# Two graph-attention layers on one core: in layer 0, the edges inside a tile of 128 nodes are summed with a 128x128 block of weights per head

## The chip, the cores and the metric

The kernel is written for one core of a Trainium2 chip. Its time is the device time of one execution in microseconds (us). The engines are named as in the profile: PE (TensorE, with its weight loads on PEld), DVE (VectorE), ACT (ScalarE), POOL (GpSimd) and SP (SyncE, which here only issues transfers). The core has 16 DMA engines.

## The reference

The input is x with 3327 rows of 1024 numbers, and a symmetric 0/1 matrix adj of 3327x3327 with ones on its diagonal; about 0.5% of it is set. Two layers follow, each with a residual and a layer norm. What layer 0 computes, with 8 heads of 128 columns:

```python
h = (x @ W).reshape(C, H, D)
alpha_src = jnp.einsum('hcd,hd->hc', h_heads, a_src)
alpha_dst = jnp.einsum('hcd,hd->hc', h_heads, a_dst)
e = alpha_src[:, :, None] + alpha_dst[:, None, :]
e = jnp.where(e >= 0, e, 0.2 * e)
e = jnp.where(adj[None] == 0, -jnp.inf, e)
attn = jax.nn.softmax(e, axis=-1)
out = jnp.einsum('hij,hjd->hid', attn, h_heads)
x = layernorm(x + out)
```

Layer 1 is the same with one head of 1024 columns, an own W, and a relu on its sum. Output: 3327x1024, float32.

## The kernel before

The nodes are cut into NT = 26 tiles of P = 128 rows (the last one is padded). A node is a *target* where its sum is formed and a *source* where its row of h is used. After the first stage a flag decides between a dense and a sparse program; this input takes the sparse one. All its stages are in an order written out by hand (`manual_schedule`): each engine runs its instructions in the order of the program, and waits only for the data and buffers that it needs.

**Projection and edge lists (L453 to L699).** For each tile, `flip` transposes x (L176), `project` multiplies it with W (L479), and `keep` copies the result out of PSUM on ACT (L491 to L496) and stores a row of HW0 = 1040 numbers per node into `h0_d`: h for 8 heads, and two factors per head (the exponentials of alpha_dst and of 0.2 alpha_dst). Between the matmuls, `pace` advances the generator `listing`, which turns the mask of adj into lists of edges, one tile a round. The steps of a round that matter here:
- `words` (L301): POOL clears the diagonal in the tile's own 128x128 block of the mask (L308), since the edge from a node to itself is handled apart; ACT counts the ones of each row by a copy of the whole mask row with an accumulator (`junk`, L311); DVE packs the mask into words (L318). It runs for the tile four rounds ahead.
- `ends` and `ends2`: PE adds up the counts (L327, L346), ACT copies the sums out (L328, L347), POOL works out the places from them.
- `keys`, `columns` (DVE): the columns of the ones in each row.
- `places`: ACT computes `away` (L384, L385), DVE compares it to form `place` (L391, L392), a matrix of ones which puts each edge into a slot.
- `give` (PE, L401, L411) multiplies with `place`; `take` (ACT, L423 to L428) copies the result out; `sources` (DVE, L436 to L450) makes of it `idx`, the source row of each slot; `tgt` is the target of each slot, `re` a factor of the target per head. A slot with no edge gets an index beyond the table, which the gather drops; for tiles 0 and 1 it gets row 0 instead, so that the buffers hold finite numbers.

**Layer 0 (class `Layer0`, pipelined by `pipeline`).** Each tile has NB = 17 gathers of 128 rows (L803, POOL, indirect DMA): EB = 4 batches of NG = 4, each of the four for 32 of the tile's targets, and one for what is left (`end`). Five `src` buffers hold the batches in turn. For a batch, `weights` computes on DVE and ACT the weight of each slot and head (L865 to L868) and multiplies it with the one-hot rows `oh` of its targets into `e` (L870; three buffers); `sums` multiplies `e` with the gathered rows on PE (L898, for the last batch L882), and the one-hot rows with the weights for the denominators (L907, L886). While the sums of batch b run, `weights` of the next is issued ahead of them, and the same batch of the next tile is fetched behind them. The edge of a node to itself is added by `own`: its weight `es` is computed on DVE (L845 to L847), ACT scales the tile's own rows with it (L850), and PE adds the scaled rows through an identity matrix (L890). `finish` divides (L918 to L924), applies the layer norm, computes the scores of layer 1 (L931), and stores the row into `y_d`.

**Layer 1 (class `Target`)** gathers from `y_d` with the same `idx`, sums with L993, and multiplies with W afterwards (L1025).

Of the kernel before, what the change touches and what calls it, by code (L numbers as in the profile page):

```python
# [9 lines left out]
F32 = mybir.dt.float32  # L10
BF16 = mybir.dt.bfloat16
U8 = mybir.dt.uint8
# [7 lines left out]
P = 128  # L20
# [6 lines left out]
def kernel(  # L27
# [84 lines left out]

    cnt = const.tile([P, NT, 3], F32, name="cnt")
    loop = const.tile([P, NT], F32, name="loop")


    idx = const.tile([P, NT, NB], I32, name="idx")
# [162 lines left out]
    class Edges:  # L280
# [20 lines left out]
        def words(self, ad, junk):  # L301

            sbuf, ph, t = self.ph.sbuf, self.ph, self.t
            own = ad[:, t * P : (t + 1) * P].bitcast(mybir.dt.int8)
            nc.gpsimd.affine_select(  # L308
                out=own, in_=own, pattern=[[1, P]], compare_op=OP.not_equal, fill=0.0, base=0, channel_multiplier=-1
            )  # L310
            nc.scalar.activation(junk, ad, AF.Copy, accum_out=self.deg)  # L311
            self.deg_b = sbuf("deg_b", [P, 1], 4, dt=BF16)
            nc.scalar.activation(self.deg_b, self.deg, AF.Copy)
            w = ad.bitcast(I32)
            for n in range(3):
                m = WD >> n
                half = sbuf(f"wd{n}", [P, m], 4 if n == 2 else 1, dt=I32)
                nc.vector.scalar_tensor_tensor(  # L318
                    half, w[:, m:], 1 << n, w[:, :m], op0=OP.logical_shift_left, op1=OP.bitwise_or
                )  # L320
# [132 lines left out]
    with ExitStack() as own, tc.manual_schedule():  # L453
# [112 lines left out]
        nc.vector.memset(masks[4], 0.0)  # L566
        nc.vector.memset(masks[4][:, :1], 1.0)
        junk = pool.tile([P, NP], U8, bufs=1, name="junk")
        junk_h = pool.tile([P, DH], BF16, bufs=1, name="junk_h")
        def score_column(k):  # L570

# [171 lines left out]
    def sparse(own):  # L743
# [12 lines left out]
        way = bank("E", [P, HALF], "way")  # L756
        ident_b = pool.tile([P, P], BF16, name="ident_b")
        nc.vector.tensor_copy(ident_b, ident)
        none_b = pool.tile([P, 1], BF16, name="none_b")
        nc.vector.memset(none_b, 0.0)  # L760
        io_t = ph.iota([P, P], [[1, P]], "io_t", base=1)
# [35 lines left out]
        listed = {}  # L797
        last = nc.gpsimd.to_reg(NP - 1)

        def gather(table, w, t, b):  # L800
            s = srcs[(t * EB + b) % NS] if b < EB else ends[t % 2]
            for g in range(NG if b < EB else 1):
                nc.gpsimd.indirect_dma_start(  # L803
                    out=s[:, g, :w], out_offset=None, in_=table[:, :],
                    in_offset=bass.IndirectOffsetOnAxis(ap=idx[:, t, b * NG + g : b * NG + g + 1], axis=0),
                    bounds_check=last, oob_is_err=False,
                )
# [6 lines left out]
        def marks(t):  # L814
# [4 lines left out]
            nc.vector.tensor_tensor(  # L819
                parts[0], io_t[:, :GT].unsqueeze(1).to_broadcast([P, m, GT]),  # L820
                tgt[:, t, :m].unsqueeze(2).to_broadcast([P, m, GT]), OP.is_equal,
            )
            nc.vector.tensor_scalar(parts[1], io_t, tgt[:, t, m:], None, op0=OP.is_equal)
            return parts

        class Layer0:
# [4 lines left out]

            def prepare(self):
                self.re = listed.pop(self.t)
                self.oh, self.oh2 = marks(self.t)
# [17 lines left out]
            def begin(self):  # L852
                self.acc = [bank("A", [P, 4, DH], "acc") for _ in range(2)]

            def fetch(self, b):
                self.src[b] = gather(h0_d, HW0, self.t, b)

            def weights(self, b):

# [16 lines left out]
            def sums(self, b):  # L876
# [9 lines left out]
                    nc.tensor.matmul(self.den, self.oh2, w[:, 0, :], start=False, stop=True)  # L886
                    return

                if b in (1, 2):
                    nc.tensor.matmul(  # L890
                        self.acc[b - 1].rearrange("p h d -> p (h d)"), ident, self.h[:, (b - 1) * HALF : b * HALF],
                        start=False, stop=False,
                    )
                elif b == 3:
                    nc.tensor.matmul(self.acc[0][:, 0, :1], ident_b, none_b, start=False, stop=False)
                for h in range(H):
                    for g in range(NG):
                        nc.tensor.matmul(  # L898
                            self.acc[h // 4][g * GT : (g + 1) * GT, h % 4, :], e[:, g, h, :], rowsof[:, g, h, :],
                            start=first and h % 4 == 0, stop=False,  # L900
                        )
# [38 lines left out]
        class Target:  # L940
# [5 lines left out]
            def prepare(self):  # L946
# [7 lines left out]
                self.oh, self.oh2 = marks(t)  # L954
                self.res = ys[t % 3]
                nc.sync.dma_start(self.res, y_d[t * P : (t + 1) * P, :])

# [8 lines left out]
                nc.vector.tensor_tensor(es[:, :1], es[:, 1:], loop[:, t : t + 1], OP.mult)  # L966

            def fetch(self, b):
                self.src[b] = gather(y_d, HW, self.t, b)

            def begin(self):
                self.acc = [bank("A", [P, CUTS[1]], "acc1") for _ in range(3)]
# [259 lines left out]
```

## Time and profile before

| | us |
|---|---|
| Time, median of 3 runs | 1955.56 (1948.99 to 1957.19) |
| The profiled execution, its own time | 1903.19 |
| Span of the profile | 1901.5 |
| Busy: PE / PEld / DVE / ACT / POOL | 1518.5 / 902.4 / 1146.6 / 546.6 / 1030.2 |
| Gathers of layer 0 on POOL (L803, 416 of them) | 441.1 |
| Sums of layer 0 on PE (L898) | 278.5 |
| Projection on PE (L479) | 402.3 |
| First gather of layer 0, first gather of layer 1 | at 482.3, at 1198.6 |

The times of all rows come from one profiled execution, which was 52 us shorter than the median of the runs. A group of instructions is shown as: line, engine, operation, written tile, read tiles, partitions x elements, count; then busy time in us and mean duration in ns; then the engine's idle time just before them and what ended most of it. A wait is shown as: who waited, for whom, us in total, how often, the longest.

### The profile page before, as it was taken

What the parts mean: (1) busy time and instruction counts of PE and PEld (TensorE: products, weight loads), DVE (VectorE), ACT (ScalarE), POOL (GpSimd) and SP (SyncE); (2) the same over time, 40 slices, a digit from 0 to 9 for tenths busy, and PEclk for the clock granted to TensorE, in tenths of its full rate; (3) what the DMA queues carried; (4) which work ended last, traced back from release to release, by engine and by line L of the source; (5) the groups of instructions that cost most, each with busy time, mean ns of one, the idle gap of its engine ahead of it and who ended that gap; (6) DMA issues with size and microseconds to landing.
All of it is one profiled execution on the core that took longest, in us unless ns stands there. A gap on an engine that the chain in (4) does not pass through costs nothing.

```text
span 1901.5 us, 38079 instructions
## 1 busy us (share of the span) xinstructions
PE 1518.5 (80%) x14663; PEld 902.4 (47%) x14663; DVE 1146.6 (60%) x3058; ACT 546.6 (29%) x1422; POOL 1030.2 (54%) x1391
## 2 busy tenths in 40 slices
PE   8799999999266555656556565399999999999997
PEld 5465556666255554545545454144444444444443
DVE  6699999986386665666666666244444444444442
ACT  5544455542022222222222222012222212222220
POOL 4322222220576666676676764677766667666650
PEclk9899999999678777787788877699999999999999
DMA  7656455411899999999999997899999999999980
GB/s 184 101 133 131 100 99 99 88 62 39 325 373 404 396 392 394 366 405 392 386 392 389 394 376 273 332 398 410 400 372 382 380 378 369 359 371 373 366 326 33
DMA packets 171068, 567.76 MB, mean 299 GB/s; under 512 B 27690, under 2 KB 34346, under 8 KB 170878
## 3 DMA queue, kind: packets, MB, share of 16 engines
q0 software_dynamic: 131056, 455.68, 67.6%
q1 hardware_dynamic: 39822, 109.56, 15.4%
q8 instruction: 118, 1.93, 0.4%
q14 instruction: 72, 0.59, 0.1%
HBM read 578.85 MB, written 42.97 MB: 327 GB/s over the span
## 4 chain that ended last, share of the span: by engine, by line
PE 52%; DMA 24%; DVE 12%; ACT 6%; issue 4%; POOL 2%; SPq 0%; DVEq 0%; ACTq 0%; POOLq 0%
DMA src<-h_d,idx 20%; PE mm L1025 20%; PE acc L993 12%; PE mm L479 12%; DVE e L870 3%; PE acc L898 3%; ACT junk L311 3%; PE tr L176 2%; POOL src L803 2%; DMA src<-y_d,idx 2%; DVE pr L931 1%; PE acc L882 1%; DMA wt<-in_L_gnn_W_dram 1%; ACT xT L179 1%; PE xp L411 1%
## 5 line engine op out<-in xcount | busy, mean ns | idle before, releaser
L803 POOL DMA_INDIRECT src<-h_d,idx x416 | 441.1, 1060 | 209.1 <-PE acc L898 58.0
L803 POOL DMA_INDIRECT src<-y_d,idx x416 | 415.7, 999 | 221.6 <-PE acc L993 96.3
L898 PE MATMUL acc<-src,e 128*32 128x128 f32 x6656 | 278.5, 337 | 253.6 <-DVE e L870 253.5
L479 PE MATMUL mm<-wt,xT 128*128 128x347 f32 (+1 forms) x1248 | 402.3, 469 | 3.3 <-DMA wt<-in_L_gnn_W_dram 2.9
L1025 PE MATMUL mm<-wt,xT 128*128 128x512 f32 x832 | 383.3, 604 | 0.8 <-DVE o L1028 0.8
L898 PEld LDWEIGHTS acc<-src,e 128*32 128x32 f32 x6656 | 234.8, 137 | 311.3 <-DVE e L870 284.3
L479 PEld LDWEIGHTS mm<-wt,xT 128*128 128x128 f32 x1248 | 228.3, 192 | 106.0 <-issue 4.2
L1025 PEld LDWEIGHTS mm<-wt,xT 128*128 128x128 f32 x832 | 152.2, 190 | 199.5 <-issue 179.1
L993 PE MATMUL acc<-src,es 128*32 128x342 f32 (+1 forms) x2496 | 206.2, 464 | 33.8 <-DVE es L984 31.0
L870 DVE TENSOR_TENSOR e<-oh,way 128x1024 f32<-128x1024 f32 x130 | 158.7, 1221 | 63.2 <-ACT w L868 62.8
L993 PEld LDWEIGHTS acc<-src,es 128*32 128x32 f32 x2496 | 71.6, 111 | 158.6 <-issue 112.9
L868 ACT ACTIVATE w<-way 128x32 f32<-128x32 f32 (+1 forms) x130 | 24.6, 189 | 407.7 <-DVE way L866 395.6
L1028 DVE SCALAR_TENSOR_TENSOR o<-mm,y 128x512 f32<-128x512 f32 x52 | 35.9, 691 | 166.2 <-PE mm L1025 166.2
L1007 ACT ACTIVATE z<-y,ri 128x342 f32<-128x342 f32 (+1 forms) x78 | 39.5, 570 | 313.9 <-DVE ri L1003 313.9
L865 DVE TENSOR_TENSOR way<-src,re 128x32 f32<-128x32 f32 x104 | 20.8, 200 | 175.1 <-DMA src<-h_d,idx 157.6
L179 ACT ACTIVATE xT<-tr 128x512 f32<-128x512 f32 x104 | 59.4, 596 | 151.0 <-PE tr L176 150.9
L981 DVE TENSOR_TENSOR way<-way,src 128x128 f32<-128x128 f32 x104 | 31.1, 299 | 90.0 <-ACT way L951 44.2
L850 ACT ACTIVATE own<-own,es 128x128 f32<-128x128 f32 x208 | 63.6, 388 | 57.4 <-DVE es L847 57.4
L311 ACT ACTIVATE junk<-ad 128x3328 uint8<-128x3328 uint8 x26 | 78.4, 3014 | 2.5 <-POOL ad L308 2.5
L882 PE MATMUL acc<-end,e 128*128 128x128 f32 x416 | 67.7, 328 | 13.3 <-DVE e L870 13.3
L296 POOL CAST mvs<-r 128x8 bf16<-128x8 f32 x26 | 6.0, 232 | 122.8 <-ACT r L295 122.8
L335 POOL TENSOR_TENSOR place_of<-cnt 128x1 f32<-128x1 f32 x26 | 4.9, 190 | 121.0 <-ACT cnt L328 101.5
(188 smaller groups left out, 1959.7 us busy)
## 6 DMA issues: line engine op xcount, KB each, us to landing
h_d<-ht SPq DMA_DIRECT2D x26, 520.0 KB
own<-h_d SPq DMA_DIRECT2D x26, 520.0 KB
y_d<-y SPq DMA_DIRECT2D x26, 514.0 KB
y<-y_d SPq DMA_DIRECT2D x26, 514.0 KB
x<-in_x_dram SPq DMA_DIRECT2D x25, 512.0 KB
y<-in_x_dram SPq DMA_DIRECT2D x25, 512.0 KB
out_dram<-o SPq DMA_DIRECT2D x25, 512.0 KB
ad<-in_adj_dram POOLq DMA_DIRECT2D x25, 415.9 KB
```

Of the source, the lines that this page charges most:

```text
L176: nc.tensor.transpose(tr[:, k, :], src[:, (4 * g + k) * P : (4 * g + k + 1) * P], ident)
L179: nc.scalar.activation(part, tr, AF.Copy)
L311: nc.scalar.activation(junk, ad, AF.Copy, accum_out=self.deg)
L479: nc.tensor.matmul(acc, xT[t][:, k, :], wt[:, k, CUTS0[c] : CUTS0[c + 1]], start=k == 0, stop=k == KT - 1)
L803: nc.gpsimd.indirect_dma_start(out=s[:, g, :w], out_offset=None, in_=table[:, :], in_offset=bass.IndirectOffsetOnAxis(ap=idx[:, t, b * NG ...
L850: nc.scalar.activation(hn, hn, AF.Copy, scale=es[:, n : n + 1])
L870: nc.vector.tensor_tensor(e, oh.unsqueeze(2).to_broadcast([P, ng, H, wide]), wp.unsqueeze(3).to_broadcast([P, ng, H, wide]), OP.mult,)
L882: nc.tensor.matmul(self.acc[h // 4][:, h % 4, :], e[:, 0, h, :], rowsof[:, 0, h, :], start=False, stop=h % 4 == 3,)
L898: nc.tensor.matmul(self.acc[h // 4][g * GT : (g + 1) * GT, h % 4, :], e[:, g, h, :], rowsof[:, g, h, :], start=first and h % 4 == 0, stop= ...
L993: nc.tensor.matmul(self.acc[c][to, :m], es[:, g, :], s[:, g, CUTS[c] : CUTS[c + 1]], start=b == 0, stop=b == EB,)
L1007: nc.scalar.activation(z[:, cut], self.res[:, cut], AF.Copy, scale=ri[:, 1:2])
L1025: nc.tensor.matmul(acc, xT[:, k, :], wt1[:, k, half], start=k == 0, stop=k == KT - 1)
```

## The change

The edges inside a tile, the one from each node to itself among them, leave the gathers of layer 0 and are summed from the tile's own rows of h, which are loaded in any case. For this:
- in `words`, ACT copies the tile's 128x128 block of the mask into `block` (bf16) before POOL clears the diagonal;
- in `ends`, PE transposes `block`, and ACT stores it as `near` (sources by targets, one byte each), which stays in SBUF;
- `outside` finds the slots whose source lies in the tile (DVE, four small operations), sets their target to 0, so that no one-hot row matches them, and for tiles from 2 on moves their index beyond the table;
- `own` and `own_half` make per head a block `el` of weights: PE transposes the broadcast factor of the targets, four heads at a time, ACT forms Relu(r a - b), DVE adds b and multiplies with `near`; `el` takes one of the three `e` buffers;
- `sums` of batch 1 has 8 matmuls with `el` over the own rows for the sums and 8 with a column of ones for the denominators, instead of L890 on batches 1 and 2; `finish` no longer adds `es`.

Layer 1 keeps its lists. The core of the diff:

```diff
@@ words
-            own = ad[:, t * P : (t + 1) * P].bitcast(mybir.dt.int8)
+            own = ad[:, t * P : (t + 1) * P]
+            self.block = sbuf("block", [P, P], 4, dt=BF16)
+            nc.scalar.activation(self.block, own, AF.Copy)
+            own = own.bitcast(mybir.dt.int8)
             nc.gpsimd.affine_select(
...
@@ ends
+            tb = self.ph.bank("T", [P, P], "tb", BF16)
+            nc.tensor.transpose(tb, self.block, self.ph.same)
+            nc.scalar.activation(near[:, self.t, :], tb, AF.Copy)
             op = self.ph.bank("T", [P, 1], "op")
...
+        def outside(t):
+
+            inside = sbuf("inside", [P, NB], 2)
+            nc.vector.tensor_scalar(inside, idx[:, t, :], float(t * P), None, op0=OP.is_ge)
+            nc.vector.scalar_tensor_tensor(
+                inside, idx[:, t, :], float((t + 1) * P), inside, op0=OP.is_lt, op1=OP.mult
+            )
+            to = sbuf("far_t", [P, NB], 3)
+            nc.vector.scalar_tensor_tensor(to, inside, 0.0, tgt[:, t, :], op0=OP.is_equal, op1=OP.mult)
+            rows_of = idx[:, t, :]
+            if t > 1:
+                rows_of = sbuf("far_i", [P, NB], 3, dt=I32)
+                nc.vector.scalar_tensor_tensor(
+                    rows_of, inside, float(NONE), idx[:, t, :], op0=OP.mult, op1=OP.add
+                )
+            far[t] = rows_of, to
...
         def get_edges(t):
+            for n in (0, 1) if t == 0 else (t + 1,):
+                if n < NT:
+                    outside(n)
...
@@ Layer0.own
-                es = self.es = sbuf("es0", [P, H], 2)
-                nc.scalar.activation(es, sd0[:, t, 0, :], AF.Exp, scale=1 - SLOPE)
-                nc.vector.tensor_tensor(es, es, h[:, D : D + H], OP.mult)
-                nc.vector.tensor_tensor(es, es, h[:, D + H :], OP.max)
-                nc.vector.tensor_scalar(es, es, loop[:, t : t + 1], None, op0=OP.mult)
-                for n in range(H):
-                    hn = h[:, n * DH : (n + 1) * DH]
-                    nc.scalar.activation(hn, hn, AF.Copy, scale=es[:, n : n + 1])
+                r, nb = sbuf("es0", [P, H], 2), sbuf("nb0", [P, H], 2)
+                nc.scalar.activation(r, sd0[:, t, 0, :], AF.Exp, scale=1 - SLOPE)
+                nc.vector.tensor_scalar(nb, h[:, D + H :], -1.0, None, op0=OP.mult)
+                self.el = sbuf("e", [P, H * P], 3, "el").rearrange("p (h t) -> p h t", h=H)
+                self.rn = r, nb
+                self.own_half(0)
+
+            def own_half(self, g):
+                t, h, e = self.t, self.h, self.el
+                r, nb = self.rn
+                tr = bank("T", [P, 4, P], "tr")
+                for n in range(4):
+                    nc.tensor.transpose(
+                        tr[:, n, :], r[:, 4 * g + n : 4 * g + n + 1].to_broadcast([P, P]), ident
+                    )
+                for n in range(4 * g, 4 * g + 4):
+                    nc.scalar.activation(
+                        e[:, n, :], tr[:, n % 4, :], AF.Relu, bias=nb[:, n : n + 1], scale=h[:, D + n : D + n + 1]
+                    )
+                    nc.vector.scalar_tensor_tensor(
+                        e[:, n, :], e[:, n, :], h[:, D + H + n : D + H + n + 1], near[:, t, :],
+                        op0=OP.add, op1=OP.mult,
+                    )
...
@@ Layer0.sums
-                if b in (1, 2):
-                    nc.tensor.matmul(
-                        self.acc[b - 1].rearrange("p h d -> p (h d)"), ident, self.h[:, (b - 1) * HALF : b * HALF],
-                        start=False, stop=False,
-                    )
-                elif b == 3:
+                if b == 1:
+                    for h in range(H):
+                        nc.tensor.matmul(
+                            self.acc[h // 4][:, h % 4, :], self.el[:, h, :], self.h[:, h * DH : (h + 1) * DH],
+                            start=False, stop=False,
+                        )
+                elif b > 1:
                     nc.tensor.matmul(self.acc[0][:, 0, :1], ident_b, none_b, start=False, stop=False)
...
+                if b == 0:
+                    self.own_half(1)
...
+                if b == 1:
+                    for h in range(H):
+                        nc.tensor.matmul(
+                            self.den[:, h : h + 1], self.el[:, h, :], one, start=False, stop=False
+                        )
...
@@ Layer0.finish
-                nc.vector.tensor_tensor(ri, self.den, self.es, OP.add)
-                nc.vector.reciprocal(ri, ri)
+                nc.vector.reciprocal(ri, self.den)
```

The gathers of layer 0 take their indices from `far[t][0]`, its one-hot rows their targets from `far[t][1]`; those of layer 1 stay with `idx` and `tgt`.

More of the change, by code (lines that the diff above doesn't have):

```diff
@@ L114 @@
     loop = const.tile([P, NT], F32, name="loop")
+    near = const.tile([P, NT, P], U8, name="near")
     idx = const.tile([P, NT, NB], I32, name="idx")
@@ L568 @@
         junk = pool.tile([P, NP], U8, bufs=1, name="junk")
+        ph.same = pool.tile([P, P], BF16, bufs=1, name="same")
+        nc.vector.tensor_copy(ph.same, ident)
         junk_h = pool.tile([P, DH], BF16, bufs=1, name="junk_h")
@@ L758, in sparse @@
         nc.vector.tensor_copy(ident_b, ident)
+        one = pool.tile([P, 1], F32, name="one")
+        nc.vector.memset(one, 1.0)
         none_b = pool.tile([P, 1], BF16, name="none_b")
@@ L798, in sparse, with gather @@
         last = nc.gpsimd.to_reg(NP - 1)
-        def gather(table, w, t, b):
+        far = {}
+        def outside(t):
[13 more added lines that the diff above has]
+            far[t] = rows_of, to
+        def gather(table, w, t, b, rows_of):
             s = srcs[(t * EB + b) % NS] if b < EB else ends[t % 2]
@@ L804, in gather @@
                     out=s[:, g, :w], out_offset=None, in_=table[:, :],
-                    in_offset=bass.IndirectOffsetOnAxis(ap=idx[:, t, b * NG + g : b * NG + g + 1], axis=0),
+                    in_offset=bass.IndirectOffsetOnAxis(ap=rows_of[:, b * NG + g : b * NG + g + 1], axis=0),
                     bounds_check=last, oob_is_err=False,
@@ L810, in get_edges, with marks @@
         def get_edges(t):
+            for n in (0, 1) if t == 0 else (t + 1,):
+                if n < NT:
+                    outside(n)
             listed[t] = sbuf("re", [P, NB, H], 3)
             nc.sync.dma_start(listed[t], re_d[t])
-        def marks(t):
+        def marks(to):
             m = NB - 1
@@ L820, in marks @@
                 parts[0], io_t[:, :GT].unsqueeze(1).to_broadcast([P, m, GT]),
-                tgt[:, t, :m].unsqueeze(2).to_broadcast([P, m, GT]), OP.is_equal,
+                to[:, :m].unsqueeze(2).to_broadcast([P, m, GT]), OP.is_equal,
             )
-            nc.vector.tensor_scalar(parts[1], io_t, tgt[:, t, m:], None, op0=OP.is_equal)
+            nc.vector.tensor_scalar(parts[1], io_t, to[:, m:], None, op0=OP.is_equal)
             return parts
@@ L833, in prepare @@
                 self.re = listed.pop(self.t)
-                self.oh, self.oh2 = marks(self.t)
+                self.oh, self.oh2 = marks(far[self.t][1])
                 self.y = ys[self.t % 3]
@@ L855, in fetch @@
             def fetch(self, b):
-                self.src[b] = gather(h0_d, HW0, self.t, b)
+                self.src[b] = gather(h0_d, HW0, self.t, b, far[self.t][0])
             def weights(self, b):
@@ L953, in prepare @@
                 )
-                self.oh, self.oh2 = marks(t)
+                self.oh, self.oh2 = marks(tgt[:, t, :])
                 self.res = ys[t % 3]
@@ L968, in fetch @@
             def fetch(self, b):
-                self.src[b] = gather(y_d, HW, self.t, b)
+                self.src[b] = gather(y_d, HW, self.t, b, idx[:, self.t, :])
             def begin(self):
```

## The prediction

> **What bounds the kernel now.** I read the slices of the page first (part 2; 40 slices of 47.5 us).
>
> ```profile
> PE   8799999999266555656556565399999999999997
> DVE  6699999986386665666666666244444444444442
> PEclk9899999999678777787788877699999999999999
> DMA  7656455411899999999999997899999999999980
> ...
> L898 PE MATMUL acc<-src,e 128*32 128x128 f32 x6656 | 278.5, 337 | 253.6 <-DVE e L870 253.5
> L870 DVE TENSOR_TENSOR e<-oh,way 128x1024 f32<-128x1024 f32 x130 | 158.7, 1221 | 63.2 <-ACT w L868 62.8
> ```
>
> Three stages show: up to about 480 us PE and DVE are full (projection and edge lists); from 482 to 1198 us the DMA row is full (layer 0); after that PE and DMA both are (layer 1). The change touches the first two. The busy-time windows give their sizes (columns: busy us of PE, PEld, DVE, ACT, POOL with counts, clock, DMA share, GB/s).
>
> ```profile
> 100.00:460.00 360.00, 350.21 (x2387) 215.61 (x2385) 326.13 (x917) 172.71 (x477) 81.23 (x377) 1.00 0.46 97
> 500.00:1150.00 650.00, 392.20 (x7637) 327.16 (x7635) 414.67 (x996) 157.25 (x463) 441.75 (x419) 0.79 1.01 390
> ```
>
> In layer 0 the DMA share is 1.01 at 390 GB/s while PE has 40% and DVE 36% free: bytes bound it. In projection PE is 97% busy and DVE 91%. The waits from 60 to 460 us tell what PE's last 3% wait for, and the timeline of one round of the edge lists why.
>
> ```profile
> PEld L411 <- DVE place L391: 29.6, 21, 7.9
> ...
> PE xp L411 <- DVE place L391: 18.0, 14, 7.3
> ...
> DVE place L391 <- ACT away L384: 16.1, 19, 4.2
> ```
> ```profile
> 209.04 0.29 POOL L308 TENSOR_SCALAR_AFFINE_SELECT ad<-ad 128x128 int8<-128x128 int8 x1
> ...
> 209.66 0.57 DVE L318 SCALAR_TENSOR_TENSOR wd<-ad 128x416 int32<-128x416 int32 x1
> ...
> 209.95 0.22 ACT L428 ACTIVATE tgt<-xp 128x1 f32<-128x1 f32 x1
> 210.00 3.02 ACT L311 ACTIVATE junk<-ad 128x3328 uint8<-128x3328 uint8 x1
> ...
> 213.14 0.20 ACT L313 ACTIVATE deg_b<-cnt 128x1 bf16<-128x1 f32 x1
> ...
> 214.00 0.73 ACT L384 ACTIVATE away<-io_q,place_of 128x512 f32<-128x512 f32 x1
> ...
> 214.76 0.49 DVE L391 TENSOR_SCALAR place<-away,cnt 128x512 bf16<-128x512 f32 x1 [0.64 <-ACT away L384]
> ```
>
> One round is a closed loop: PE's placing matmuls (L411, L401), ACT's copies (to L428), ACT's row count over the mask (`junk`, 3.02), ACT's `away`, DVE's `place`, PE's next L411. POOL's clearing of the diagonal (L308) is off it: it ended 0.67 us before ACT and 0.33 before DVE (L318) needed the mask. PE waits for `place` in 14 of 25 rounds and is just in time in most others, so what lengthens this loop lengthens the stage.
>
> [...] granted clock 0.79 in layer 0, and 64 matmuls of L898 took 3.64 us after a gap of 4.04 us, 1.95 us without one. More PE work in layer 0 should therefore partly pay for itself.
>
> **Layer 0: bytes removed.** The reference's mask has 53,496 edges off the diagonal; 2,120 of them (4.0%) lie within a tile. Tiles 0 and 1 keep theirs as gathers (rows_of is changed for t > 1 only), so 1,960 rows of 4,160 bytes go: 8.15 MB, at 390 GB/s **20.9 us**. That an index past the end moves nothing shows in the page: software_dynamic moved 455.68 MB, while 56,576 slots a layer at 4,160 and 4,112 bytes would be 468 MB without the mask loads. The number of gathers on POOL stays 17 a tile; each takes 0.99 and 0.30 to the next, 21.9 us a tile.
>
> A tile now takes 26.3 us (mean step of L918) and would take 25.5. Work per tile on the others:
> - PE: now 392.2/650 x 26.3 = 15.9. Added: eight f32 transposes (L176: eight in 1.03 warm, 1.97 cold), 1.5; eight block matmuls (L882, same shape, 67.7/26) 2.6; eight sums of one column with full weights (L886, 0.29 each) 2.3. Removed: L890 twice, 1.1. Sum 21.2, 83% of 25.5.
> - DVE: now 16.8. Added: eight masked multiplies (L924, eight in 2.16) 2.2, four small operations in `outside` (L447, 0.17) 0.7, one for nb 0.2; removed four of some 0.2. Sum 19.1.
> - ACT: eight Relu instead of eight scaled copies (L850, 2.44), even.
>
> All stay under 25.5, so the DMA hides them, but the coupling is tighter. DVE's half 0 waits for transposes queued behind the last tile's sums, half 1 for those behind sums(0); `el` takes one of three `e` buffers, so the `e` of batch 3 waits for sums(1). Sums(1) ends some 5 us later (4 matmuls of half 1, den, and DVE's 1.2), and with it the refill of its src buffer. The chain shows gathers of 9 to 14 us from issue to landing against some 6.3 us for a batch, so one to two batches are queued: 5 us fit once a tile, if recovered. Uncovered are the start (from 520 to 545 us the chain runs through DVE pr L773 and e L870) and the last tile (own lands at 1166 and everything follows it): 2 us each. Layer 0: -20.9 + 4 = **-17**; bounds -21 and, with half the gain lost to drained queues, -6.
>
> **Projection: a wait added.** ACT copies the block before POOL clears the diagonal, and ACT's `junk` and DVE's L318 still wait for POOL. Now L308 starts only after ACT's tgt copies. Price: block copy 0.29 (L425, same tile, 0.285), hand-over 0.08 (L328 ends at 250.28, POOL's L335 starts at 250.36), L308 0.29, hand-over 0.08: 0.74 us in which ACT has nothing else. Queued behind on ACT: junk, deg_b, `away`, and often the copies of project (L496). On DVE, L318 moves to 210.74, by 1.08; `sources` and `places` are behind it; on POOL, the next mask load and factors, both early. In the shown round `away` moves by 0.74, DVE is ready at 215.20, earlier than `away` at 215.47, and place comes 0.74 later. So I read 22 rounds from 85 to 413 us: +0.7 in most, +0.3 in three where DVE was the later, 0.85 to 1.3 in four where L318 stood first. Sum 17. Start-up has two words in a row on ACT (65.8, 69.0): +0.7. The bf16 transpose in `ends` is on PE inside the loop: L346's row beside it costs under 0.1, L176's transpose 0.13; 26 x 0.1 = 2.6. The `near` copy (0.29) falls where ACT waits 2 to 4 us for L327; cnt goes 0.3 later, and POOL has 2.4 to spare before L346. Projection: **+20**; from below 8 (if the last rounds, where PE is 100% busy, and the rounds just in time absorb it), from above 28 (if DVE's later start adds to ACT's). Layer 1 and the tables of ACT are unchanged: 0.
>
> **Sum.** 1903.19 (the profiled execution, span 1901.5) - 17 + 20 = 1906. The runs shown have a median of 1955.56, 2.7% above it; I carry the difference over: 1958.6, said as 1958. Where those runs lose 52 us no view shows; if to slower transfers, the saving is a little larger.
>
> **Rivals.**
> 1. The added wait is hidden (*faster*). For it: several rounds have PE just in time, and PE is 100% busy from 400 to 460. Against it: 18.0 us of waits for `place`. With +5 in projection: -17 + 5 = -12, some 1943. Chance 0.22.
> 2. The gain of layer 0 is half lost (*slower*): later refills of src drain the DMA queue at each tile's start. Decides if sums(1) runs over by more than the queue's 1 to 2 batches (6 to 12 us). For it: own work crosses PE, ACT, DVE and PE twice, and POOL needs 5.2 us to issue a batch. Against it: DVE waits 156.9 us for src in this stage, 6.3 a tile. -6 + 20 = +14, 1970. Chance 0.22.
> 3. PE bounds layer 0 (*slower*): at a clock as low as in the cold bursts (3.64 for 1.95) 21.2 becomes over 25.5 from a factor of 1.2 on. At 27.5 a tile: 24 x 1.2 = +29, with +20: 2005. Against it: the clock should rise. Chance 0.11.
> 4. That indices are not dropped: unlikely, as existing empty slots are marked in the same way; +24, in rival 2's chance.
>
> **Numbers.** The likeliest case, 0.45, is no change: 1958, its own range 1947 to 1968. A measurement of this kernel tells from no change about 0.5%, 10 us. Faster by more 0.22, within 0.43, slower by more 0.35. The range 1938 to 1986 takes in rivals 1 and 2 and the bounds (-21 + 8 = -13 and -6 + 28 = +22) with some width for the runs, and leaves out rival 3.
>
> **What would show it.** Right: projection ends near 500 us instead of 480; ACT idle before `junk` of 0.4 to 0.5 by POOL in each round, and L411's wait for `place` up by some 15 us; layer 0 from first gather to the first of layer 1 some 699 us instead of 716, DMA share still 1.0, clock above 0.79. Wrong: a DMA share below 0.97 in layer 0 (rivals 2, 3), PE over 95% there (3), or projection longer by under 8 us (1).

## The result and the profile after

The changed kernel takes 2035.87 us (median; 2030.36 to 2038.57), the kernel before beside it 1956.38 (1948.99 to 1958.43): a ratio of 1.0392, 95% interval 1.0365 to 1.0419. It is slower by 79.5 us, outside the predicted range (1938 to 1986).

The slices and the sums of layer 0 on the page after, as shown of before (40 slices, now of 50.8 us):

```profile
PE   8799999998478878888878878369999999999997
...
DVE  6688888886576766675576666424444444444342
...
PEclk9899999999678788787787887769999999999999
DMA  7555445410989999999999999499999999999980
...
L948 PE MATMUL acc<-src,e 128*32 128x128 f32 x6656 | 375.9, 325 | 126.9 <-issue 114.4
```

The group L948 is L898 of before: the same 6,656 matmuls. Before, PE stood idle ahead of them for 253.6 us and waited for DVE's `e`, which waited for rows. Now 114.4 of its 126.9 us of idle time end on "issue": on nothing that the profile shows. The busy time rose from 278.5 to 375.9 us while the mean of one went from 337 to 325 ns: the matmuls did not become longer, they overlap less. The DMA row still shows nines in layer 0; the windows below tell more.

The windows of the kernel after (columns as before):

```profile
100.00:460.00 360.00, 336.12 (x2256) 206.57 (x2254) 309.52 (x865) 178.30 (x503) 84.92 (x380) 0.99 0.45 96
500.00:1150.00 650.00, 502.83 (x7276) 403.53 (x7278) 417.76 (x1074) 149.86 (x404) 379.67 (x372) 0.79 0.93 336
```

In layer 0 the transfers went from 390 to 336 GB/s, and the share from 1.01 to 0.93. Bytes are no longer the bound. The gathers by `src` give the stages (first and last start in us):

```profile
L834 POOL DMA_INDIRECT src<-y_d,idx x416: 984/991/1487, 1307.8 to 1973.0; - x139
...
L834 POOL DMA_INDIRECT src<-h_d,idx x32: 986/990/2012, 507.1 to 558.6; - x32
```

Layer 0 ran from 507.1 to 1307.8, 801 us, against 716 before; the projection ended 25 us later. The waits of layer 0 in the kernel after (507 to 1308 us) put the largest one on PE's weight loads:

```profile
PEld acc L948 <- issue: 210.9, 337, 2.0
...
PE acc L948 <- issue: 114.4, 233, 1.8
DVE el L896 <- issue: 110.2, 18, 9.1
```

PE's timeline shows what such a wait looks like. These are the weight loads inside one batch's sums; from 858 to 861 us the granted clock is 1.00:

```profile
857.30 0.18 PEld L948 LDWEIGHTS acc<-src,e 128*32 128x32 f32 x3 [0.52 <-issue]
858.03 0.19 PEld L948 LDWEIGHTS acc<-src,e 128*32 128x32 f32 x5 [0.54 <-issue]
858.75 0.14 PEld L948 LDWEIGHTS acc<-src,e 128*32 128x32 f32 x2 [0.54 <-issue]
859.49 0.11 PEld L948 LDWEIGHTS acc<-src,e 128*32 128x32 f32 x1 [0.60 <-issue]
860.20 0.19 PEld L948 LDWEIGHTS acc<-src,e 128*32 128x32 f32 x5 [0.60 <-issue]
860.92 0.11 PEld L948 LDWEIGHTS acc<-src,e 128*32 128x32 f32 x1 [0.54 <-issue]
```

PE does a handful of weight loads with their matmuls in 0.2 us, stands for 0.55, and goes on, each 0.73 us after the last. Over the stage, some 160 such steps are 0.7 to 0.8 us apart and some 50 twice that (how many depends on where a pause is taken to begin); three to four weight loads of each are recorded, and some records are missing. The data of all 32 matmuls were there, since one `e` and one `src` serve them all. DVE's "issue" ahead of `el` is of another kind: in the timeline ACT's `el` begins 0.49 us earlier (at 629.78, DVE's at 630.27) after a wait of its own for PE, and DVE follows it. Only PE's waits have no visible cause.

Of the 79.5 us, 25 are thus the projection's. The other 55 lie in layer 0 and behind it. How they divide can't be read: the kernel before has no trace at its 1956 us, and its profile of 1903 us has next to none of these waits. Set 2 below has both kernels with the waits.

### The profile page after: what moved, and what is told of

It reads as the page before. It is cut to its first block, busy times and chain, and to the rows that moved or that the text cites. A ratio compares the mean times of both kernels' runs of the same rounds, so it can differ in the third digit from the quotient of the medians.

```text
span 2033.2 us, 40346 instructions
## 1 busy us (share of the span) xinstructions
PE 1737.7 (85%) x15651; PEld 1060.5 (52%) x15651; DVE 1214.8 (60%) x3292; ACT 575.7 (28%) x1474; POOL 1020.8 (50%) x1391
## 3 DMA queue, kind: packets, MB, share of 16 engines
q0 software_dynamic: 131056, 447.53, 64.7%
q8 instruction: 125, 2.05, 0.4%
## 4 chain that ended last, share of the span: by engine, by line
PE 72%; issue 9%; ACT 7%; DVE 6%; DMA 3%; POOL 2%; another core or an unknown queue 2%; SPq 0%; POOLq 0%; DVEq 0%; ACTq 0%
PE mm L1081 17%; PE acc L948 17%; PE mm L487 12%; PE acc L1049 11%; PE acc L931 4%; PE acc L940 3%; ACT junk L316 3%; PE tr L178 2%; PE den L965 2%; PE tr L889 1%; POOL src L834 1%; DMA wt<-in_L_gnn_W_dram 1%; DMA src<-h_d,idx 1%; PE den L959 1%
## 5 line engine op out<-in xcount | busy, mean ns | idle before, releaser
L834 POOL DMA_INDIRECT src<-h_d,far_i x384 | 391.7, 1020 | 287.9 <-PE acc L948 117.8
L948 PE MATMUL acc<-src,e 128*32 128x128 f32 x6656 | 375.9, 325 | 126.9 <-issue 114.4
L487 PE MATMUL mm<-wt,xT 128*128 128x347 f32 (+1 forms) x1248 | 409.7, 475 | 3.4 <-DMA wt<-in_L_gnn_W_dram 2.3
L948 PEld LDWEIGHTS acc<-src,e 128*32 128x32 f32 x6656 | 250.2, 129 | 227.7 <-issue 210.9
L1049 PE MATMUL acc<-src,es 128*32 128x342 f32 (+1 forms) x2496 | 212.3, 466 | 39.4 <-DVE es L1040 26.9
L896 DVE SCALAR_TENSOR_TENSOR el<-el,own,near 128x128 f32<-128x128 f32 x208 | 70.6, 351 | 205.3 <-issue 110.2
L893 ACT ACTIVATE el<-tr,nb,own 128x128 f32<-128x128 f32 x208 | 78.3, 457 | 263.3 <-PE tr L889 156.4
L931 PE MATMUL acc<-end,e 128*128 128x128 f32 x416 | 81.8, 375 | 2.4 <-DVE e L919 2.0
L1057 DVE TENSOR_TENSOR ri<-acc,es 128x1 f32<-128x1 f32 x26 | 4.1, 158 | 125.6 <-PE acc L1049 112.8
L931 PEld LDWEIGHTS acc<-end,e 128*128 128x128 f32 x416 | 74.9, 278 | 4.8 <-DVE e L919 2.1
```

What stands on the lines that cost most here:

```text
L487: nc.tensor.matmul(acc, xT[t][:, k, :], wt[:, k, CUTS0[c] : CUTS0[c + 1]], start=k == 0, stop=k == KT - 1)
L834: nc.gpsimd.indirect_dma_start(out=s[:, g, :w], out_offset=None, in_=table[:, :], in_offset=bass.IndirectOffsetOnAxis(ap=rows_of[:, b * NG ...
L893: nc.scalar.activation(e[:, n, :], tr[:, n % 4, :], AF.Relu, bias=nb[:, n : n + 1], scale=h[:, D + n : D + n + 1])
L896: nc.vector.scalar_tensor_tensor(e[:, n, :], e[:, n, :], h[:, D + H + n : D + H + n + 1], near[:, t, :], op0=OP.add, op1=OP.mult,)
L931: nc.tensor.matmul(self.acc[h // 4][:, h % 4, :], e[:, 0, h, :], rowsof[:, 0, h, :], start=False, stop=h % 4 == 3,)
L948: nc.tensor.matmul(self.acc[h // 4][g * GT : (g + 1) * GT, h % 4, :], e[:, g, h, :], rowsof[:, g, h, :], start=first and h % 4 == 0, stop= ...
```

## The experiments

They ran in five sets. Each set has its own runs of the kernel before, and kernels are compared within a set, because the kernel before took 1898.52, 1987.57, 1901.48, 1902.76 and 1899.60 us in them; sets 2 and 3 were on the same chip, a quarter of an hour apart. Stages in us, from the profiles by first gathers:

| Run | Set | Ratio (95%) | Projection to | Layer 0 | Rest |
|---|---|---|---|---|---|
| e1, before | 1 | 1 | 479.3 | 710.7 | 704.7 |
| e3, `el` in a buffer of its own | 1 | 1.0054 (1.0037 to 1.0071) | 504.1 | 696.8 | 702.8 |
| e4, block copied by POOL | 1 | 0.9951 (0.9935 to 0.9968) | 488.1 | 699.2 | 700.6 |
| e6, before | 2 | 1 | 482.3 | 779.5 | 735.4 |
| e5, after | 2 | 1.0370 (1.0348 to 1.0391) | 505.6 | 813.0 | 739.6 |
| e7, lists only | 2 | 0.9999 (0.9982 to 1.0016) | 482.7 | 769.4 | 732.8 |
| e8, block, all gathered | 2 | 1.0352 (1.0317 to 1.0387) | 501.1 | 815.5 | 740.5 |

Only set 2 shows PE's waits; the profile of the recorded result shows them too. In the texts below, theory C is that PE's instructions come late while transfers fill the DMA engines, and that the change gives PE more of them; the other theories are named in each text.

### Set 1: the parts that the prediction had priced

**e1: the kernel before.** 

> The kernel before, unchanged, with a profile on the chip of the other runs of this set. The first profile of it was 52 us shorter than its timed runs. Theory A (layer 0 of the changed kernel is bound by PE, whose work grew and whose instruction supply stalls): here a step of layer 0 stays 26 to 27 us and PE's sums wait for DVE's e, not for nothing (issue). Rival (stalls of PE with no waited-for engine are there before the change as well, and the first profile was a lucky one): the profile shows 100 us and more of L898 waiting on issue and a step near 28 us.

Measured: 1896.42 us. Its window 560 to 1140 us in layer 0:

```profile
560.00:1140.00 580.00, 350.48 (x7042) 293.54 (x7046) 370.01 (x906) 147.14 (x430) 399.90 (x381) 0.82 1.01 394
```

That is the picture of the first profile: the transfers bound it. None of PE's matmuls waits on "issue" in it.

**e2: more PE instructions.** The kernel before with

```diff
+                if b:
+                    for _ in range(13 if b < 3 else 12):
+                        nc.tensor.matmul(self.acc[0][:, 0, :1], ident_b, none_b, start=False, stop=False)
```

> The kernel before, with 37 more matmuls of one bf16 column per tile in layer 0 (the L895 kind, adding zeros), so that PE issues about as many instructions per tile as in the changed kernel (348 matmuls for 311) with little added busy time (under 0.1 us each, some 3 us a tile, where PE waits 9.5 us a tile for e). Theory A1 (PE is held by the supply of its instructions): a step of layer 0 goes from 26.3 towards 29 us, the time up by 50 us or more. Theory A2 (PE is held by its busy time alone): up by less than 10 us, since the wait for e takes the 3 us in.

The loops add 38 matmuls in a tile (988 in the trace, for 26 tiles), so 76 instructions with their weight loads, and all of them in layer 0. The texts here and below that say 37 and 74, or "each layer", are off by that.

Measured: ratio 0.9997 (0.9988 to 1.0007). In the window from 560 to 1140 us 861 of the added matmuls take 32.59 us of PE's busy time, 0.04 us each. With the transfers as the bound, 76 more instructions of PE in a tile are free.

**e3: `el` not in `e`'s buffers.** The kernel after with

```diff
-                self.el = sbuf("e", [P, H * P], 3, "el").rearrange("p (h t) -> p h t", h=H)
+                self.el = sbuf("z", [P, D], 3, "el").rearrange("p (h t) -> p h t", h=H)
```

> The changed kernel with el in buffers of its own (those that layer 1 uses for z), so that it no longer takes one of the three e buffers. Theory A (PE-bound): the step of layer 0 stays at 29.4 us, the time within 10 us of the changed kernel (2035). Rival B (the coupling through the e buffers holds DVE and so PE): the step falls by 2 us or more, the time by 50 us or more.

Measured: 1.0054; layer 0 696.8 us, 14 less than e1 and only 2 less than e4, where `el` shares `e`'s buffers. The sharing costs next to nothing.

**e4: POOL copies the block.** The kernel after with

```diff
-            nc.scalar.activation(self.block, own, AF.Copy)
+            nc.gpsimd.tensor_copy(self.block, own)
```

> The changed kernel with the copy of the 128x128 block made on POOL, in front of its clearing of the diagonal, instead of on ACT. By the prediction's step for projection ACT no longer waits for POOL between tgt and junk: the stage gives back 14 to 17 of the 20 us, the time falls to some 2018 to 2021. Rival (the added length of projection is PE's transposes and the T buffers): less than 5 us come back. Layer 0 is not touched and should stay at 29.4 us a step.

Measured: 0.9951, faster than the kernel before. The projection ends at 488.1 and not at 504.1 as in e3, whose projection is that of the changed kernel: ACT's place in the order was worth 16 us. Layer 0's gain of 11.5 us stays.

### Set 2: the changed kernel where PE waits

**e5 and e6: both kernels again.** 

> The changed kernel, unchanged. In the set before, the kernel before took 1898.5 and the changed kernel with the block copied on POOL 1889.3, so Theory C (the large loss of the recorded result, 2035.87 against 1956.38, needs a chip or a condition in which PE lacks instructions in layer 0; without it the prediction's sum holds) expects 1905 beside a before of 1898, ratio 1.000 to 1.008, and L948 waiting on issue for under 10 us; in the other condition 1.035 to 1.043, with 200 us of that wait, and a before of some 1956. Theory A (PE-bound by its own work on every chip): ratio near 1.04 beside any before.

> The kernel before, with a profile on the same chip as the run above. If that run shows the stalls of PE, this one tells what they cost the kernel before: Theory C expects its L898 to wait on issue too, for less (50 us or more), and a step of layer 0 of 27.5 to 28.5 us; if the run above shows none, 26.2 us a step and under 20 us on issue.

Measured: 1.0370. The same window of the kernel before (e6) and of the changed one (e5), and the waits of e6 in it:

```profile
560.00:1140.00 580.00, 430.99 (x6346) 294.66 (x6347) 342.30 (x837) 135.74 (x398) 357.69 (x346) 0.84 0.97 359
```
```profile
560.00:1140.00 580.00, 467.41 (x6667) 370.86 (x6668) 369.41 (x954) 138.32 (x367) 336.05 (x327) 0.80 0.94 330
```
```profile
PEld acc L898 <- issue: 237.8, 356, 1.5
...
PE acc L898 <- issue: 132.0, 302, 1.7
```

The kernel before has the waits as well: layer 0 takes 779.5 us, 69 more than in e1, with the same matmuls. The change did not make them; it meets them. (Of the 102 us between the profiles of e1 and e6, 31 lie behind layer 0; no run shows their cause.)

What bounds layer 0 is another engine here. In e6 PE is busy for 430.99 of the 580 us and idle on "issue" for 138.2; everything else that it waits for comes to 8.3. In e5 the three are 467.41, 100.9 and 6.9. And the wait for rows, which bounds e1, is nearly gone in e6. Over the whole run, first e1, then e6:

```profile
DVE way L865 <- DMA src<-h_d,idx: 162.8, 66, 7.8
```
```profile
DVE way L865 <- DMA src<-h_d,idx: 21.1, 4, 8.7
```

Of the 61 us between the profiles of e6 and e5, 23 lie in the projection, 33 in layer 0 and 4 behind. (e6's profiled execution was 11 us above its median, so by the medians layer 0 lost up to 44.)

**e7: lists without the edges inside a tile.** The kernel before with `outside` and its lists, and its old `own`. 

> The kernel before, with only the lists of layer 0 shortened as in the change: the slots inside a tile get no target and, from tile 2 on, no index. It leaves out the edges inside a tile other than the own one. The prediction's first step (8.15 MB at 390 GB/s): 20.9 us less than before, 1878 beside 1898, a step of 25.5 us. If PE's instruction supply binds, 0 to 5 us less.

Measured: 0.9999. So 8.15 MB fewer bytes and `outside` on DVE give nothing here, and cost nothing. The row packets do take longer in e6 than in e1 (an estimate from their share of the 16 engines in the window, 81.5% for 49,520 packets and 84.4% for 54,516: 153 and 144 ns each), but slower transfers that bound layer 0 would make fewer bytes worth more, not nothing.

**e8: the block, and all rows gathered.** The kernel after with

```diff
-            if t > 1:
+            if t > NT:
```

> The changed kernel with every index left in its gathers, so that the block does the in-tile sums while their rows still arrive (without a target). Where the bytes bind layer 0: 20.9 us more than the changed kernel. Where PE binds it (theory A, or C in its second condition): within 4 us of the changed kernel.

Measured: 1.0352 (1.0317 to 1.0387), the interval of e5. Its window has 341 GB/s, e5's 330: the bytes are moved again and the time is the same. The cost is that of the block and of ACT's wait; the saved bytes are worth nothing in this set.

### Sets 3 to 5: what are PE's waits?

These were to tell three causes apart beside a kernel before that waits. In all three sets it did not, so they tell what the change is worth without the waits, and leave the cause open.

**e9, e14, e18: the edit of e2 three times more.** 

> The kernel before with 37 one-column matmuls more in each tile of each layer (zeros added: the values are unchanged), 74 instructions of TensorE more a tile and about 1.5 us more of its busy time. The same edit as in the run e2, where TensorE hardly waited for its own instructions. The question is what the waits are that TensorE shows in layer 0 as waiting for nothing. Theory C (its instructions come late while the rows' transfers fill the DMA engines): on a chip where the kernel before shows 200 us or more of such waits in layer 0, the added instructions cost by their number, 74 of some 700 a tile, so 1.5 to 3 us a tile and the ratio 1.02 to 1.045. Rival (what counts is TensorE's busy time alone): 1.5 us a tile at the most where it is the bound and its waits unchanged, ratio 1.00 to 1.02, and the same as the kernel with wide matmuls. Where the kernel before has few such waits: ratio 1.00 again.

> The kernel before with 37 one-column matmuls more in each tile of each layer, 74 instructions of TensorE and about 1.5 us of its busy time more a tile (values unchanged). Without TensorE's waits: ratio 1.000, as twice before. With them: theory C (late instructions) 1.5 to 3 us a tile in layer 0, where the waits are, 40 to 80 us, ratio 1.02 to 1.04; if TensorE's busy time is what counts, under 1.02 and the same as the kernel with wide matmuls.

> The kernel before with 37 one-column matmuls more in each tile of each layer, 74 instructions of TensorE a tile (values unchanged), once more. If this chip shows the waits in the kernel before: late instructions say 1.5 to 3 us a tile in layer 0, ratio 1.02 to 1.04; if busy time alone counts, 1.00 to 1.01, since the 1.5 us fit beside the waits. Without the waits: 1.000, as three times before.

Measured: 1.0006 (0.9994 to 1.0018), 0.9996 (0.9985 to 1.0007), 0.9994 (0.9984 to 1.0005).

**e10, e15: eight wide matmuls more in a tile.** The kernel before with

```diff
+        zero_b = pool.tile([P, HALF], BF16, name="zero_b")
+        nc.vector.memset(zero_b, 0.0)
...
+                if b:
+                    for _ in range(3 if b < 3 else 2):
+                        nc.tensor.matmul(
+                            self.acc[0].rearrange("p h d -> p (h d)"), ident_b, zero_b, start=False, stop=False
+                        )
```

> The kernel before with 8 matmuls of 512 columns more in each tile of each layer (zeros added: the values are unchanged), 16 instructions of TensorE more and about 1.8 us more of its busy time a tile. Theory C: where the kernel before shows 200 us or more of waits of TensorE for nothing visible in layer 0, 16 instructions of some 700 cost 0.3 to 0.7 us a tile, and the busy time itself fits in the waits: ratio 1.00 to 1.01, clearly below the kernel with 74 short instructions. Rival (busy time counts): the same as that one or more.

> The kernel before with 8 matmuls of 512 columns more in each tile of each layer, 16 instructions of TensorE and about 1.8 us of its busy time more a tile (values unchanged). Without TensorE's waits: ratio 1.000 again. With them: theory C (late instructions) 1.00 to 1.01, clearly below the kernel with 74 short instructions; if busy time counts, the same as that kernel or more.

Measured: 0.9995 (0.9984 to 1.0006) and 0.9996 (0.9986 to 1.0006). Layer 0's window of e10 has PE at 397.88 us of 580 with 390 GB/s: 47 us more of PE than in e1, some 2.3 a tile of 27.5 (an estimate; the texts said 1.8), all beside the transfers. (These 8 matmuls too are in layer 0 alone.) The number of instructions and busy time could not be told apart.

**e11, e13, e17: half of the rows.** The kernel after with

```diff
+                nc.vector.memset(rows_of[:, : NB - 1 : 2], NONE)
```

for the tiles from 2 on. 

> The changed kernel, in which every other column of gathers of tiles 2 and on carries no index in layers 0 and 1, so that about half of the rows' bytes do not move; the matmuls, the descriptors' preparation and everything else stay. It leaves the edges of those columns out of its sum. If TensorE's waits for nothing visible come from competition with the rows' transfers, they vanish, and a step of layer 0 falls from 29 us to what TensorE and POOL need, 22 to 24 us: the time of layer 0 down by 140 to 200 us against the changed kernel. If TensorE's instructions come late for a reason of its own (their number, the order of its waits), the waits of 200 us or more stay, and the step stays at 28 to 29 us. If the step falls to 26 with the waits still there, both have a share.

> The changed kernel in which every other column of gathers of tiles 2 and on carries no index in layers 0 and 1, so that about half of the rows' bytes do not move (the edges of those columns are left out of its sum). Without TensorE's waits the same kernel gave 0.973 of the kernel before. If this chip shows the waits in the kernel before: competition with the rows' transfers says that they vanish here, layer 0 takes about 660 us as it does without them, and the ratio is 0.94 or less; a cause within TensorE (its number of instructions) says that they stay, layer 0 takes 780 us or more, and the ratio is 1.01 or more. Without the waits in the kernel before: 0.973 again.

> The changed kernel in which every other column of gathers of tiles 2 and on carries no index in layers 0 and 1 (the edges of those columns are left out of its sum), once more. If this chip shows TensorE's waits in the kernel before: competition of its instructions with the rows' transfers says that few of them are left here, ratio 0.95 or less; a cause within TensorE says that 200 us of them stay in layer 0, ratio 1.01 or more. Without the waits in the kernel before: 0.973, as twice before.

The line changes the lists of layer 0 only, not of both layers as the texts have it: layer 1 takes its indices from `idx`, and what follows layer 0 takes 702.5 us in e11, as in e3 (702.8).

Measured: 0.9729 (0.9707 to 0.9750), 0.9739 (0.9713 to 0.9764) and 0.9749 (0.9718 to 0.9780). The kernel before of these sets was as quick as in set 1, and the profiles beside it (e9, e10, e12) show next to no waits of PE for nothing visible in L898 or L948, so competition could not be seen. But the run measures something else, the cover. Layer 0's window in e11:

```profile
560.00:1140.00 580.00, 436.41 (x8718) 405.28 (x8717) 479.47 (x1256) 178.73 (x476) 433.36 (x412) 0.89 0.81 249
```

The transfers are no bound any more (0.81), and still layer 0 takes 642.9 us, 24.7 a tile, against 700.5 (26.9) in e12 of the same set. The busiest engine, DVE, has 479.47 of 580 us, or 20.4 of the 24.7; PE waits for DVE's products more than for anything else:

```profile
PE acc L949 <- DVE e L920: 65.0, 38, 4.2
```

So with half of the rows the changed kernel needs 24.7 us a tile, and all rows add only 2.2 us to that.

**e12, e16: the edit of e4 again.** 

> The changed kernel with the copy of the own block in POOL's own order instead of in ScalarE's, as in the run e4. It takes ScalarE's wait out of the projection: the first gather again at about 488 us instead of 504 on any chip. On a chip with few of the waits in layer 0: ratio 0.995 again. On one with 200 us or more of them: theory C says that the matmuls of the block cost their 33 us or so in layer 0 in either version, so 16 us under the changed kernel, ratio 1.025 to 1.03, and still slower than the kernel before; if the ratio is below 1.01 there, the projection's wait and not TensorE is what made the changed kernel slower.

> The changed kernel with the copy of the own block in POOL's own order. Without TensorE's waits: ratio 0.993 to 0.995, as twice before. With them: the first gather at 488 us and not 504, layer 0 as long as that of the changed kernel there, so 16 us below the changed kernel's ratio of 1.037: 1.025 to 1.03. If below 1.01, the projection's wait and not TensorE made the changed kernel slower there.

Measured: 0.9933 (0.9917 to 0.9950) and 0.9941 (0.9918 to 0.9964), as in e4. In e12 the sums of layer 0 read

```profile
L948 PE MATMUL acc<-src,e 128*32 128x128 f32 x6656 | 258.6, 320 | 124.7 <-DVE e L919 123.6 <-issue 0.7
```

Beside the line of the page after: 0.7 us of "issue" instead of 114.4.

### What stays open

PE's waits are shown, their cause is not. Seen: they come with the time and not with the chip alone (sets 2 and 3). They are in the sums of layer 0, where the kernel before runs 24 instructions of PE a us in e1 (7042 + 7046 in 580 us), with a full DMA row. A full DMA row alone does not make them: e1 moves 394 GB/s without them, e6 359 with them. Nor does a lower granted clock: 0.84 in e6's window, 0.82 in e1's.

One reading is that PE's instructions come late. The page of the kernel after counts 125 packets of 2.05 MB in the queue that it calls instruction, 16.4 KB each. Their number goes with that of PE's instructions: in the window from 560 to 1140 us there are 55 packets beside 14,088 records of PE and PEld in e1, 51 beside 12,693 in e6, 52 beside 13,335 in e5 and 63 beside 16,186 in e4, so 249 to 257 records to a packet. But the packets themselves are no slower where PE waits. In that window, first e1, then e6 (packets, MB, share of the 16 engines):

```profile
q8 instruction: 55, 0.90, 0.6%
```
```profile
q8 instruction: 51, 0.84, 0.6%
```

From the shares that is 1.0 and 1.1 us a packet (an estimate). And PE stops after a handful of loads, while a packet goes with some 250 of its instructions (an estimate from the counts above). Whether PE's instructions came late at all, the traces do not show. What made the condition of the recorded result and of set 2 differ from that of the others, no run shows.

## Why the prediction failed, point by point

- **The projection: right.** Predicted +20 (8 to 28), measured +23 to +25. The waits of the kernel after from 60 to 460 us hold the predicted places:

```profile
PEld L419 <- DVE place L399: 44.0, 22, 8.3
...
PE xp L419 <- DVE place L399: 30.8, 19, 7.3
...
ACT junk L316 <- POOL ad L313: 9.6, 24, 0.4
```

and one round of its timeline shows the four steps:

```profile
237.32 0.35 ACT L311 ACTIVATE block<-ad 128x128 bf16<-128x128 uint8 x1
...
237.75 0.29 POOL L313 TENSOR_SCALAR_AFFINE_SELECT ad<-ad 128x128 int8<-128x128 int8 x1 [1.30 <-ACT block L311]
...
238.07 2.98 ACT L316 ACTIVATE junk<-ad 128x3328 uint8<-128x3328 uint8 x1 [0.40 <-POOL ad L313]
```

ACT idles 0.40 us ahead of `junk` in 24 rounds (0.4 to 0.5 was said), the start of `junk` is 0.75 after that of the block's copy (0.74 was said), and PE's wait for `place` grew from 29.6 to 44.0 on the weight loads and from 18.0 to 30.8 on the matmuls (some 15 was said). Rival 1, that it is hidden, is out. e4 has 16 of it less than e3 by one line.

- **Layer 0 where the transfers bound it: near.** Predicted -17 (-21 to -6). e3 took 696.8 us from first gather to first gather and e4 699.2, against 710.7: -14 and -11.5. That the forecast's 699 was met is luck in part, since it started from 716. The changed kernel itself was not run in that condition; e3, which differs from it in one buffer, came out at 1.0054, +8.5 us, where the sum said +3.

- **Layer 0 as recorded: wrong, and this is the step that failed.** "All stay under 25.5, so the DMA hides them" took the 390 GB/s of one profile, 52 us shorter than the runs, as the bound of all runs. "I carry the difference over" treated that gap as a constant, although, in its own words, "where those runs lose 52 us no view shows". In the set that shows such a loss, two thirds of it (69 of 102 us, e6 against e1) is layer 0, where PE stands; so it is not a constant: it takes the cover away. With it the saved bytes give 0 (e7) instead of 20.9, and the block's work costs 33 to 44 us (e5 against e6, e8 about the same) instead of 4. In the sum's own terms it is PE's 21.2 us a tile. The profile after has, from 560 to 1140 us,

```profile
560.00:1140.00 580.00, 468.15 (x6790) 374.02 (x6789) 377.83 (x974) 141.27 (x374) 337.79 (x333) 0.80 0.94 335
```
```profile
PE acc L948 <- issue: 88.9, 186, 1.1
```

With its other lines PE is idle on "issue" for 101.5 us and waits only 5.5 for anything else. In a tile of 30.8 us (801/26) that is 24.9 busy and 5.4 idle, 30.3 together, where the sum had 21.2 and no such idle time. (The 24.9 are stretched too: without the waits PE has 19.0 for the same work, in e12.) That the timed runs of the kernel before at 1956 us had PE's waits as well is likely from e6, but no trace of them shows it.

- **The cover was thinner than the sum.** This holds without the waits too. PE's 21.2 us a tile was, if anything, high there (e12's window from 500 to 1150 has 459.84 of 650 us, so 19.0 in a step of 26.9; the removed L890 were 60.3/26 = 2.3 and not 1.1). But a tile with half of its rows still takes 24.7 (e11), though its busiest engine has 20.4, since the engines wait for each other; the sum took the busiest engine for the limit.

- **The rivals.** The mark given for rivals 2 and 3, a DMA share below 0.97, came true (0.93). Rival 3, "PE bounds layer 0", named the right engine, with 27.5 a tile against 30.8 measured. Its cause, a clock that falls, did not come: the granted clock is 0.79 from 500 to 1150 us, as before, and its mark, PE over 95% busy, did not show (502.83 of 650 us), since part of PE's time is idle. Without the waits the granted clock is higher with the change (0.86 from 560 to 1140 us in e12 and e3, against 0.82 in e1), as the prediction had it. The rival had a chance of 0.11, and the range left it out. Rival 2, a drained queue through the shared `e` buffers, is not supported where the transfers bind: e3 takes the sharing away for 2 us, and layer 0 gains 11.5 to 14 us there, not 6. Rival 4, rows not dropped, is out: the queue of the gathers (software_dynamic) moved 455.68 MB on the page before and 447.53 on the page after, the 8.15 less that were counted.

## What to carry to other kernels

Where the profiled execution is a few per cent off the runs, the gap is a finding to be explained before anything is priced on that profile: the bound that hides an edit may not be there in the runs that count. Ask how thick the cover is by the chain of one tile, not by its busiest engine; one run with half of the transfers left out, like e11, measures it. And where an edit puts one engine's step between two of another's, look for an engine that has the buffer in hand already: copying the block on POOL, which clears the same buffer next, turned +8.5 us (e3) into -9.2 us (e4) beside the same runs of the kernel before. That version is slightly faster than the kernel before in three sets (0.9951, 0.9933, 0.9941); in the recorded condition it was not run, and 16 us off 2035.87 would still leave it some 3% slower there (an estimate).

## What was not expected of the hardware

PE can stand still inside one batch of matmuls, with all data in place, in steps of 0.73 us: 211 us on the weight loads of layer 0 in the changed kernel, 238 us within 580 us of it in the kernel before (e6). The kernel before took 1987.57 us on one chip in the set whose profiles show such waits, and 1901.48 us on the same chip a quarter of an hour later, in a set whose profiles show next to none. In the busy time of PE they hide: its share in layer 0's window rose from 350.48 to 430.99 us of 580 (e1 to e6) with a tenth fewer matmuls recorded, which reads as a fuller PE and is an emptier one.
